# A mask addition moved from VectorE to TensorE, and a layer norm fused on VectorE, in a four-layer decoder with a computed order

## The chip, the cores and the metric

The kernel runs on one core of a Trainium2 chip. A core has a matrix engine (TensorE, PE in the profile, with its weight loads as PEld), VectorE (DVE), ScalarE (ACT), GpSimd (POOL) and SyncE (SP), which here only issues transfers. Each engine works off its own queue in order, and they meet at semaphores. Operands lie in SBUF, an on-chip memory of 128 partitions; matmuls write to PSUM, which GpSimd does not use here.

The metric is the device time of one execution in microseconds, as the median of several runs.

## What is computed

A stream of 128 batches of 64 tokens of width 128 passes four layers. Each layer adds an attention over a context and then a feed-forward part, both on a layer-normed stream:

```python
x = x + _L0_xattn_ref(_layernorm(x), ctx, ctx, mask_if1, ...)   # 16 heads of 8, mask per query and key
x = x + _L0_ffn_ref(_layernorm(x), ...)                          # 8 experts, all computed, gated
x = x + _L1_xattn_ref(ctx, _layernorm(x), mask_bk0, ..., rel_bias)
x = x + _L1_ffn_ref(_layernorm(x), ...)
x = x + _L2_xattn_ref(...)                                       # products without softmax
x = x + _L2_ffn_ref(...)                                         # one of 7 experts a token
x = x + _L3_xattn_ref(_layernorm(x), ctx, ctx, mask_bss, gamma, beta)
x = x + _L3_ffn_ref(...)                                         # attention with mixed weights
```

The change touches two places. In layer 0's attention the scores of masked pairs are set to a very negative value ahead of the softmax:

```python
scores = jnp.einsum('bhqd,bhkd->bhqk', query, key_) / np.sqrt(D_K)
scores = jnp.where(mask == 0, jnp.float32(NEG), scores)
attn = jax.nn.softmax(scores, axis=-1)
```

Layer 3's attention ends in a layer norm with a learned scale and shift:

```python
xhat = (x - mu) * jax.lax.rsqrt(var + EPS)
return xhat * gamma + beta
```

## The kernel before

**Groups and parts.** The 128 batches are cut into 16 groups of 8 batches (512 tokens). A group's stream lies in a tile of 128 partitions by 4 by 128, `xg[g]`, that stays in SBUF from start to end. For each group there are parts: `attention(g, 0)`, `l0f`, `attention(g, 1)`, `l1f`, `attention(g, 2)`, `route`. Layer 2's feed-forward part sorts tokens by expert (`table`, `block`, `shared`, `gather`) in two halves, groups 0 to 11 and 12 to 15. Then come `l3x` (layer 3's attention) for each group, `mix` for each four groups and `l3f` for each group.

**The order.** The program does not issue its instructions in the order in which it is written. Each piece of work is an `op` with an engine (or two to choose from), a planned duration, the tiles that it reads and writes, and a priority. `Plan.order` runs a model of five queues: for each engine it takes, among the ops that could start within `WINDOW` of the earliest one, the one of lowest priority number, and gives tiles their buffers as they come free. Where an op may go to two engines, `ALT` weighs the duration that it has on each. The number of buffers of each kind is in `spec`. A table `PRI` adds an offset to the priority of each kind of op. The result is a fixed order of each engine's queue. The planned durations are no more than the planner's: on the chip an instruction takes what it takes, and waits for semaphores.

**Layer 0's attention** (`attention`). A mask tile of 128x256 int32 is loaded (`load_mask`); POOL turns it into 0 or a very negative number in a tile `mb` (L933). Two projections give queries and keys. The keys are spread into a block-diagonal tile `kbd` by transfers (`fill_kbd`). For each half `v` of a group, `scores` (L733 on) issues 16 matmuls into the one PSUM tile `S` (four banks, 128x2048), L755. Two DVE instructions then add the mask while they move the scores to the SBUF tile `s` (L967). Then come the row maximum on DVE (`maximum`, L779), its subtraction on POOL (`shift`, L794), exp on ACT (`exp_`, L785), transposes on PE (`attend`, L809), the copy out of PSUM (`copy_out`, L593 on ACT or L591 on DVE), the product with the values (L821) and the normalisation on DVE (`normalise`, L837 to L845). `out_proj` (L888, L893) adds the outcome to the stream.

For layer 1, `scores` already has a way to add a mask on PE: it issues eight matmuls of a row of ones with the mask in bf16 (L743) ahead of the others, which then accumulate onto them.

**Layer 0's feed-forward part** (`l0f`) multiplies with all experts (L1068) and sums them on DVE (L1078). **Layer 1's** (`l1f`) has L1125 and L1144 on PE.

**Layer 3.** `l3x` computes scores, softmax and values for a group, then the statistics of the result (`stats`, L536 and L538), the reciprocal deviation on POOL (`pow_rs`, L544 and L545), and the norm: four tensor_scalar on DVE (L1562), a multiplication by gamma on POOL (L1570), the addition of beta to the stream (`add_row`, L610), and the addition of the product to the stream on POOL (L1574), and the stream's statistics for the next part. `gather` holds scalar_tensor_tensor instructions of 128x128 (L1464). `mix` picks experts for four groups (`choose`, `weigh`). `l3f` loads a pair of weight tiles for each batch (`load`; L1734 is the matmul that waits for them), and runs an attention much like layer 0's; for its second half, ACT copies the scores out of PSUM (L1786).

`route` ranks tokens: `r2` to `r5` are sequences of small DVE instructions (`r3` is L1211 to L1213), between `r3` and `r4` stands a count on PE (L1220).

Of the kernel before, what the change touches and what calls it, by code (L numbers as in the profile page):

```python
# [20 lines left out]
P = 128  # L21
# [44 lines left out]
SKEW, SKEW3, ALT, WINDOW = 15.0, 12.0, 1.160527449, 0.268996472  # L66
# [5 lines left out]
    "block0 block <lambda> 4": -4, "block0 block tr 0": 37, "block0 dma fn 4": 30.5,  # L72
    "block0 swiglu <lambda> 0": 3.5, "block0 swiglu <lambda> 1": 35.5, "block0 swiglu <lambda> 2": -1,
    "block0 swiglu down 0": 20, "block1 block <lambda> 1": 13.5, "block1 block <lambda> 4": -12.5,
    "block1 block tr 0": -22.5, "block1 dma fn 4": 71, "block1 swiglu <lambda> 0": 4,
    "block1 swiglu <lambda> 1": 41, "block1 swiglu <lambda> 2": -32, "block1 swiglu down 0": 1,
    "gather0 gather <lambda> 3": 3.5, "gather0 gather fn 2": 6.5, "gather0 stats fn 2": -0.5,
    "gather1 gather <lambda> 3": 78, "gather1 gather fn 2": 29.5, "gather1 stats fn 2": -3.5,
    "l0f copy_out fn 1": 3, "l0f l0f <lambda> 0": 9, "l0f l0f <lambda> 1": 9.5, "l0f l0f <lambda> 2": -145,
    "l0f l0f acc 2": -123.5, "l0f l0f eb 0": 46.5, "l0f l0f g1 2": 43.5, "l0f l0f g2 2": 41.5,  # L80
    "l0f ln_xn fn 1": 17.5, "l0f logits fn 0": 18.5, "l0f pow_rs fn 3": -4, "l0f stats fn 2": -39,
    "l0f transpose4 fn 0": 59.5, "l1f add_row <lambda> 3": 12.5, "l1f copy_out fn 1": -43.5,
    "l1f l1f <lambda> 0": 196, "l1f l1f <lambda> 2": 55.5, "l1f l1f <lambda> 3": 48, "l1f l1f choose 2": 11.5,
    "l1f l1f down 0": 360, "l1f l1f relu 1": 32, "l1f ln_xn fn 1": -12, "l1f logits fn 0": 5, "l1f pow_rs fn 3": 7,
    "l1f stats fn 2": 0.5, "l1f transpose4 fn 0": 45.5, "l3f0 attend av 0": 41.5, "l3f0 attend tr 0": -4.5,
    "l3f0 copy_out fn 1": -52, "l3f0 dma fn 4": -9.5, "l3f0 exp_ <lambda> 1": 25, "l3f0 fill_kbd fn 4": 56,
    "l3f0 l3f <lambda> 1": 2, "l3f0 l3f <lambda> 2": 17, "l3f0 l3f <lambda> 3": 106, "l3f0 l3f b_v 3": 51.5,
    "l3f0 l3f evac 1": -131, "l3f0 l3f load 4": -2, "l3f0 l3f project 0": -36.5, "l3f0 l3f put 2": -15,
    "l3f0 maximum fn 2": 40, "l3f0 normalise fn 2": 4, "l3f0 out_proj <lambda> 2": 36, "l3f0 out_proj fn 0": 11,
    "l3f0 scores fn 0": -58, "l3f0 shift fn 3": -1, "l3f1 attend av 0": 1, "l3f1 attend tr 0": -22,  # L90
    "l3f1 copy_out fn 1": 8.5, "l3f1 dma fn 4": -3, "l3f1 exp_ <lambda> 1": 14, "l3f1 fill_kbd fn 4": -18,
    "l3f1 l3f <lambda> 1": -2, "l3f1 l3f <lambda> 2": -13.5, "l3f1 l3f <lambda> 3": 4, "l3f1 l3f b_v 3": 9.5,
    "l3f1 l3f evac 1": 12.5, "l3f1 l3f load 4": -13.5, "l3f1 l3f project 0": -58, "l3f1 l3f put 2": -8,
    "l3f1 maximum fn 2": 4, "l3f1 normalise fn 2": -2, "l3f1 out_proj <lambda> 2": 4, "l3f1 out_proj fn 0": -4.5,
    "l3f1 scores fn 0": -26, "l3f1 shift fn 3": -6.5, "l3x0 add_row <lambda> 3": 8, "l3x0 copy_out fn 1": -36,
    "l3x0 dma fn 4": 61.5, "l3x0 l3x <lambda> 1": 166, "l3x0 l3x <lambda> 2": -5.5, "l3x0 l3x <lambda> 3": -10.5,
    "l3x0 l3x av 0": 28.5, "l3x0 l3x norm 2": -21.5, "l3x0 l3x sc 0": 7, "l3x0 l3x sums 2": 33,
    "l3x0 l3x tr 0": -17.5, "l3x0 ln_xn fn 1": 14, "l3x0 pow_rs fn 3": 12, "l3x0 stats fn 2": 9,
    "l3x0 transpose4 fn 0": 15, "l3x1 add_row <lambda> 3": 3.5, "l3x1 copy_out fn 1": -38, "l3x1 dma fn 4": 97,
    "l3x1 l3x <lambda> 1": 36.5, "l3x1 l3x <lambda> 2": 8, "l3x1 l3x <lambda> 3": -2, "l3x1 l3x av 0": 13.5,  # L100
    "l3x1 l3x sc 0": 26, "l3x1 l3x sums 2": -28.5, "l3x1 l3x tr 0": 7.5, "l3x1 ln_xn fn 1": -1,
    "l3x1 pow_rs fn 3": -3, "l3x1 stats fn 2": -1, "l3x1 transpose4 fn 0": -1, "mix0 add_row <lambda> 3": 26.5,
    "mix0 copy_out fn 1": -64, "mix0 ln_xn fn 1": -3.5, "mix0 mix <lambda> 0": 54.5, "mix0 mix <lambda> 1": 18.5,
    "mix0 mix <lambda> 2": -29.5, "mix0 mix b3mm 0": 37.5, "mix0 mix choose 2": 81, "mix0 mix put 2": 27.5,
    "mix0 mix spread_ 0": 101, "mix0 mix weigh 2": -76, "mix0 pow_rs fn 3": -17.5, "mix0 transpose4 fn 0": 38,
# [29 lines left out]
    "x2 stats fn 2": -15.5, "x2 transpose4 fn 0": 29, "x2 vproj_by_batch evac 2": -93.5,  # L135
    "x2 vproj_by_batch fn 0": -44, " b2_row b2_row 2": 2.5, " dma fn 4": 497, " lambda <lambda> 0": 32.5,
    " lambda <lambda> 2": -29.5, " lambda <lambda> 3": 14.5, " rel_mm rel_mm 0": -11.5,
    " scale_bq scale_bq 2": -1.5, " setup setup 3": 2.5, " stats fn 2": -18.5, " vset vset 2": 20,
}


# [1814 lines left out]
```

## Time and profile before

| | |
|---|---|
| median of 3 runs | 1987.3 us (1986.98 to 1990.2) |
| the profiled execution, its own time | 1991.25 us |
| its span | 1989.5 us |
| mean granted TensorE clock | 0.97 |
| busy: PE | 1811.3 us, 91% of the span |
| busy: DVE | 1546.2 us, 78% |
| busy: ACT | 1084.5 us, 55% |
| busy: POOL | 1022.3 us, 51% |

Durations in the next sections come from the one profiled execution. In a line of a group of instructions, the columns are: line of the program, engine, operation, output and inputs by tile name, shapes, number, and after the bar the busy time in us and the mean of one in ns, then the engine's idle time just before them and what ended most of it. In a line of waits: engine, output and line of the one that waited, what it waited for, total us, times, and the longest. In a line of the timeline: start, length, engine, line, operation. A busy time counts moments in which anything of the group ran, so overlapping matmuls count once.

### The profile page before, as it was taken

What the parts mean: (1) busy time and instruction counts of PE and PEld (TensorE: products, weight loads), DVE (VectorE), ACT (ScalarE), POOL (GpSimd) and SP (SyncE); (2) the same over time, 40 slices, a digit from 0 to 9 for tenths busy, and PEclk for the clock granted to TensorE, in tenths of its full rate; (3) what the DMA queues carried; (4) which work ended last, traced back from release to release, by engine and by line L of the source; (5) the groups of instructions that cost most, each with busy time, mean ns of one, the idle gap of its engine ahead of it and who ended that gap; (6) DMA issues with size and microseconds to landing.
All of it is one profiled execution on the core that took longest, in us unless ns stands there. A gap on an engine that the chain in (4) does not pass through costs nothing.

```text
span 1989.5 us, 66420 instructions
## 1 busy us (share of the span) xinstructions
PE 1811.3 (91%) x27506; PEld 1306.3 (66%) x27506; DVE 1546.2 (78%) x4023; ACT 1084.5 (55%) x2032; POOL 1022.3 (51%) x1331
## 2 busy tenths in 40 slices
PE   6878999999999999999999999999999897888886
PEld 5544756665765666765666677878756676677665
DVE  5989897878798987798887865354577877988776
ACT  2544755555655564556564554344455666765664
POOL 4635745554555664457654471020388767755231
PEclk8989999999999999999999999999999999998898
DMA  6200001011011010001101012444424576545561
GB/s 187 79 13 27 27 26 30 13 30 41 19 34 46 24 35 29 27 26 50 29 25 33 22 37 84 124 136 122 119 74 124 153 237 198 173 148 167 174 196 55
DMA packets 139229, 158.73 MB, mean 80 GB/s; under 512 B 40836, under 2 KB 98096, under 8 KB 138928
## 3 DMA queue, kind: packets, MB, share of 16 engines
q1 hardware_dynamic: 134832, 146.09, 24.2%
q0 software_dynamic: 4096, 8.40, 1.4%
q8 instruction: 216, 3.54, 0.8%
q14 instruction: 85, 0.70, 0.1%
HBM read 121.66 MB, written 15.99 MB: 69 GB/s over the span
## 4 chain that ended last, share of the span: by engine, by line
PE 50%; DVE 25%; POOL 7%; issue 7%; ACT 5%; DMA 4%; SPq 2%; POOLq 0%; DVEq 0%; ACTq 0%
PE b L1353 8%; PE b L1144 6%; PE b L809 5%; DVE x L1078 4%; POOL s L794 4%; DVE mx L779 4%; PE S L755 4%; PE b L1125 4%; PE b L1382 4%; PE b L1068 3%; PE b L638 3%; PE b L1734 3%; PE b L821 2%; PE b L864 2%; DVE s L967 2%
## 5 line engine op out<-in xcount | busy, mean ns | idle before, releaser
L794 POOL TENSOR_TENSOR s<-s,mx 128x512 f32<-128x512 f32 x320 | 324.0, 1047 | 224.1 <-DVE mx L779 190.5
L593 ACT COPY p<-b 128x512 f32<-128x512 f32 x370 | 199.4, 591 | 143.2 <-PE b L809 128.2
L809 PE MATMUL b<-ident,s 128*128 128x128 f32 x1536 | 217.1, 291 | 45.9 <-ACT s L785 33.7
L785 ACT ACTIVATE s<-s 128x2048 f32<-128x2048 f32 x96 | 183.8, 1914 | 114.2 <-POOL s L794 84.2
L809 PEld LDWEIGHTS b<-ident,s 128*128 128x128 f32 x1536 | 180.2, 149 | 91.0 <-ACT s L785 55.2
L563 ACT ACTIVATE xn<-x,nmr,rstd 128x128 f32<-128x128 f32 x472 | 194.4, 487 | 26.8 <-POOL nmr L548 25.2
L1078 DVE SCALAR_TENSOR_TENSOR x<-b,gt,x 128x128 f32<-128x128 f32 x512 | 177.8, 347 | 30.5 <-PE b L1068 14.3
L544 POOL TENSOR_SCALAR ve<-mv 128x4 f32<-128x4 f32 x144 | 34.8, 242 | 319.4 <-DVE mv L538 304.8
L755 PE MATMUL S<-kbd,q 32*64 32x256 f32 x4096 | 152.8, 404 | 42.6 <-DMA kbd<-k 20.4
L1144 PEld LDWEIGHTS b<-fw,hbig 128*128 128x128 f32 x1536 | 180.6, 195 | 10.4 <-issue 9.4
L1144 PE MATMUL b<-fw,hbig 128*128 128x128 f32 x1536 | 186.3, 279 | 0.0
L779 DVE TENSOR_REDUCE mx<-s 128x32 f32<-128x2048 f32 x80 | 181.8, 2274 | 3.6 <-ACT s L1786 2.9
L1370 DVE TENSOR_TENSOR hbig<-fm,b 128x256 f32<-128x256 f32 (+2 forms) x180 | 85.4, 487 | 102.0 <-ACT fm L1365 75.1
L1134 ACT ACTIVATE hbig<-b,cols 128x512 f32<-128x512 f32 x164 | 111.3, 685 | 82.8 <-PE b L1125 81.8
L1068 PE MATMUL b<-mats,fx 128*128 128x512 f32 x256 | 140.5, 632 | 1.9 <-DVE x L1078 1.5
L545 POOL TENSOR_TENSOR rstd<-ve,mhalf 128x4 f32<-128x4 f32 x128 | 133.6, 1044 | 10.6
L755 PEld LDWEIGHTS S<-kbd,q 32*64 32x64 f32 x4096 | 82.1, 137 | 83.2 <-DMA kbd<-k 19.2
L1353 PE MATMUL b<-fx,hbig 128*128 128x256 f32 (+1 forms) x528 | 129.1, 393 | 4.7 <-ACT fx L1441 1.0
L1365 ACT ACTIVATE fm<-b 128x256 f32<-128x256 f32 (+2 forms) x180 | 76.7, 438 | 101.0 <-PE b L1353 91.9
L821 PEld LDWEIGHTS b<-p,vaug 128*32 128x32 f32 x6144 | 97.1, 111 | 50.6 <-issue 23.5
L821 PE MATMUL b<-p,vaug 128*32 128x64 f32 x6144 | 123.3, 225 | 6.5 <-issue 3.6
L1125 PE MATMUL b<-fm,fw 128*128 128x512 f32 x256 | 125.1, 606 | 0.6 <-DVE x L1078 0.3
(292 smaller groups left out, 3870.2 us busy)
## 6 DMA issues: line engine op xcount, KB each, us to landing
fw<-in_l_w SPq DMA_DIRECT2D x64, 384.0 KB
vaug<-in_l_w SPq DMA_DIRECT2D x64, 384.0 KB
hbig<-in_l_w SPq DMA_DIRECT2D x44, 544.0 KB
c<-in_ctxT SPq DMA_DIRECT2D x64, 256.0 KB
kbd<-k SPq DMA_DIRECT2D x256, 64.0 KB
q<-xs_d SPq DMA_DIRECT2D x44, 128.0 KB
ys_d<-o SPq DMA_DIRECT2D x44, 128.0 KB
x<-in_x SPq DMA_DIRECT2D x32, 128.0 KB
```

What stands on the lines that cost most here:

```text
L563: A.activation(y[:, t, :], xg[g][:, t, :], AF.Identity, bias=nmr[:, g, n], scale=rstd[:, g, n])
L593: A.copy(tl(dst), tl(b))
L755: T.matmul(ps[64 * i : 64 * i + 64, r, u * 256 : u * 256 + 256], lhsT=qT[row, 64 * b : 64 * b + 64], rhs=kbd[row, :, 64 * b : 64 * b + 64] ...
L779: V.tensor_reduce(tl(mxr), heads(y), AX.X, ALU.max)
L794: G.tensor_tensor(y, y, bc(tl(mxr)[:, h], 2, [P, n, S]), ALU.subtract)
L809: T.transpose(tl(b)[:, r * P : (r + 1) * P], tl(s)[:, c : c + P], ident)
L821: T.matmul(tl(po)[32 * r : 32 * r + 32, c : c + 64], lhsT=vaugs[kv.slot][:, w0 : w0 + 32], rhs=tl(ps[p])[:, r * P + 64 * i : r * P + 64 * ...
L1068: lambda t=t, u=u, pe=pe: T.matmul(tl(pe), lhsT=tl(xnT)[:, t * P : (t + 1) * P], rhs=mats[:, M_E0 + 4 * u : M_E0 + 4 * u + 4, :], start=Tr ...
L1078: V.scalar_tensor_tensor(xg[g][:, t, :], tl(pe)[:, e * D : (e + 1) * D], w[:, t, 4 * u + e : 4 * u + e + 1], xg[g][:, t, :], ALU.mult, ALU ...
L1125: lambda n=n, src=src, ph=ph: T.matmul(tl(ph), lhsT=fw[:, n * P : (n + 1) * P], rhs=tl(src), start=True, stop=True),
L1144: T.matmul(tl(py)[:, t * P : (t + 1) * P], lhsT=tl(hs[n])[:, t * P : (t + 1) * P], rhs=w2f[:, n, :], start=(n == 0), stop=(n == 11),)
L1353: T.matmul(tl(ps)[0:n, at : at + m], lhsT=w()[:, off + c * P : off + c * P + n], rhs=tl(xT)[:, 0:m], start=True, stop=True,)
```

## The change

Layer 0's attention, for groups 0 to 4 only (`FIRST = 5`): POOL writes the mask as bf16; `scores` first issues four matmuls of the bf16 identity with the mask (one for each bank of `S`, 512 columns each, the mask's two blocks of 64 keys repeated over four heads by the access pattern), and the 16 score matmuls accumulate onto them; one ACT copy moves the sum to SBUF in place of the two DVE additions. Groups 5 to 15 stay as they were.

Layer 3's norm: the shift by beta is issued ahead; then for each of four token blocks two scalar_tensor_tensor instructions on DVE, (y - mean) * gamma and (that) * rstd + x. The two POOL instructions go.

The planner's inputs change too: planned durations of `r2`, `r3`, `r4`, `r5`, `av`, `choose`, `evac` and the latency of `load`; `ALT`, `WINDOW`; buffer counts; and the whole table `PRI` of offsets (left out here).

```diff
+FIRST = 5
-SKEW, SKEW3, ALT, WINDOW = 15.0, 12.0, 1.160527449, 0.268996472
+SKEW, SKEW3, ALT, WINDOW = 15.0, 12.0, 1.5, 0.237474501
...
+    ident_bf = sb("ident_bf", [P, P], BF16)
...
-        "c": (2, [P, GT]), "q": (2, [P, GT]), "k": (3, [P, GT]), "o": (3, [P, GT]),
-        "xnT": (1, [P, GT]), "xn": (2, [P, GT]), "fx": (2, [P, GT]), "fm": (4, [P, GT]), "p": (5, [P, GT]),
-        "s": (2, [P, 2048]), "m": (2, [P, 256]), "mb": (3, [P, 256]), "mx": (12, [P, 32]), "tn": (1, [P, 288]),
-        "st": (4, [P, TP * 6]), "gt": (2, [P, 264]),
+        "c": (2, [P, GT]), "q": (2, [P, GT]), "k": (3, [P, GT]), "o": (2, [P, GT]),
+        "xnT": (2, [P, GT]), "xn": (2, [P, GT]), "fx": (2, [P, GT]), "fm": (4, [P, GT]), "p": (5, [P, GT]),
+        "s": (2, [P, 2048]), "m": (3, [P, 256]), "mb": (2, [P, 256]), "mx": (7, [P, 32]), "tn": (1, [P, 288]),
+        "st": (8, [P, TP * 6]), "gt": (2, [P, 264]),
...
         make_identity(nc, ident)
+        G.tensor_copy(ident_bf, ident)
...
-    def scores(q, kv, kb, v, pri, keymask=None):
+    def scores(q, kv, kb, v, pri, keymask=None, pairmask=None):
...
+            if pairmask is not None:
+                pm = tl(pairmask).bitcast(BF16)[:, 0 : TP * S].rearrange("p (t k) -> p t k", k=S)
+                for r in range(4):
+                    T.matmul(
+                        ps[:, r, :], lhsT=ident_bf, rhs=bc(pm[:, 2 * v : 2 * v + 2, :], 2, [P, 2, 4, S]),
+                        start=True, stop=False,
+                    )
...
-                            start=keymask is None,
-                            stop=keymask is None or u == 1,
+                            start=alone,
+                            stop=alone or u == 1,
...
-        op(PE, 1.05 if keymask is None else 1.25, fn, r=[q, kb, *extra], w=[sc], hold=[kv], pri=pri, mode="s")
+        alone = keymask is None and pairmask is None
+        extra = [] if alone else [pairmask if keymask is None else keymask, C]
+        op(PE, 1.05 if alone else 1.25 if pairmask is None else 2.0, fn, r=[q, kb, *extra], w=[sc], hold=[kv], pri=pri, mode="s")
...
+        on_pe = layer == 0 and g < FIRST
...
-                lambda: G.tensor_scalar(tl(mask), tl(m).bitcast(I32), 0.0, NEG, ALU.is_equal, ALU.mult),
+                lambda: G.tensor_scalar(
+                    tl(mask).bitcast(BF16)[:, 0 : TP * S] if on_pe else tl(mask), tl(m).bitcast(I32), 0.0, NEG,
+                    ALU.is_equal, ALU.mult,
+                ),
...
-            if layer == 0:
+            if on_pe:
+                op(
+                    ACT, 1.95, lambda sc=sc, s=s: A.copy(tl(s), tl(sc).rearrange("p r c -> p (r c)")),
+                    r=[sc], w=[s], pri=pri,
+                )
+            elif layer == 0:
...
-        op(DVE, 1.1 + 0.45 * m, r2, r=[C], w=[rt], pri=pri)
+        op(DVE, 1.1 + 0.65 * m, r2, r=[C], w=[rt], pri=pri)
...
-        op(DVE, 0.2 + 0.8 * m, r3, w=[rt, RUN[half]], pri=pri - 1)
+        op(DVE, 0.2 + 1.0 * m, r3, w=[rt, RUN[half]], pri=pri - 1)
...
-        op(DVE, 0.7 + 0.4 * m, r4, r=[rank, W["misc2"]], w=[rt], p=[POS[half]], pri=pri - 1)
+        op(DVE, 0.6 + 0.2 * m, r4, r=[rank, W["misc2"]], w=[rt], p=[POS[half]], pri=pri - 1)
...
-        op(DVE, 1.4 + 0.2 * m, r5, w=[rt, *WSH[g0 : g0 + m]], pri=pri)
+        op(DVE, 1.1 + 0.1 * m, r5, w=[rt, *WSH[g0 : g0 + m]], pri=pri)
...
-        op(PE, 1.0, av, r=[pT, cv], w=pos_, hold=[y], pri=pri, mode="v")
+        op(PE, 0.65, av, r=[pT, cv], w=pos_, hold=[y], pri=pri, mode="v")
...
+        add_row(g, R_BETA, pri)
+
         def norm():
             for t in range(TP):
-                V.tensor_scalar(
-                    g4(tl(y))[:, t, :], g4(tl(y))[:, t, :], mv3[:, g, t, 0:1], rs3[:, g, t : t + 1],
-                    ALU.subtract, ALU.mult,
+                y_, x_ = g4(tl(y))[:, t, :], xg[g][:, t, :]
+                V.scalar_tensor_tensor(
+                    y_, y_, mv3[:, g, t, 0:1], rows[:, R_GAMMA : R_GAMMA + D], ALU.subtract, ALU.mult
                 )
-
-        op(DVE, 1.3, norm, r=[R3, M3], w=[y], pri=pri, port=True)
-        op(
-            POOL, 1.27,
-            lambda: G.tensor_tensor(g4(tl(y)), g4(tl(y)), bc(rows[:, R_GAMMA : R_GAMMA + D], 1, [P, TP, D]), ALU.mult),
-            r=[W["rows"]], w=[y], pri=pri,
-        )
-        add_row(g, R_BETA, pri)
-        op(POOL, 1.27, lambda: G.tensor_tensor(xg[g], xg[g], g4(tl(y)), ALU.add), r=[y], w=[X[g]], pri=pri)
+                V.scalar_tensor_tensor(x_, y_, rs3[:, g, t : t + 1], x_, ALU.mult, ALU.add)
+
+        op(DVE, 1.75, norm, r=[R3, M3, W["rows"]], w=[y, X[g]], pri=pri)
...
-        op(DVE, 4.2, choose, r=[W["rows"], C], w=[sel, pg], pri=pri)
+        op(DVE, 2.7, choose, r=[W["rows"], C], w=[sel, pg], pri=pri)
...
-                op(SP, 0.95, load, r=[TAB3[g // GATE]], w=[wt], pri=pri - 1, lat=3.5, after=[*mark["l1f"], *mark["x2"]])
+                op(SP, 0.95, load, r=[TAB3[g // GATE]], w=[wt], pri=pri - 1, lat=4.3, after=[*mark["l1f"], *mark["x2"]])
...
-            op(ACT, 0.5, evac, r=[b, *VA], p=[va], hold=[kv], pri=pri, alt=[(DVE, 0.5)])
+            op(ACT, 0.6, evac, r=[b, *VA], p=[va], hold=[kv], pri=pri, alt=[(DVE, 0.5)])
```

## The prediction

> **What bounds the kernel now.** I read three views. First the busy time of each engine by stretch, for the span is not one regime. Columns: stretch and its length, busy us of PE, PE weight load, DVE, ACT, POOL (records in brackets), granted TensorE clock, DMA share, GB/s.
>
> ```profile
> 33.00:200.00 167.00, 133.71 (x1785) 79.26 (x1781) 152.70 (x412) 81.39 (x131) 88.96 (x126) 0.90 0.18 53
> 200.00:1450.00 1250.00, 1207.92 (x17307) 852.29 (x17306) 956.72 (x2390) 669.85 (x1237) 599.23 (x777) 0.99 0.16 47
> 1450.00:1820.00 370.00, 318.08 (x5035) 247.20 (x5035) 306.11 (x963) 229.51 (x483) 270.42 (x348) 0.95 0.53 161
> 1820.00:1989.50 169.50, 128.84 (x3089) 108.92 (x3083) 118.49 (x213) 95.41 (x169) 50.00 (x54) 0.91 0.46 146
> ```
>
> From 200 to 1450 us PE is busy 96.6% of the time: it is the bound, and what another engine does there is worth little. From 33 to 200 us it is the other way round: DVE 91%, PE 80%, ACT 49%. In the last 540 us nobody is full (PE 83%, DVE 79%).
>
> Second, the chain that ended last, its pieces added up by engine for each stretch. From 33 to 200 us: DVE 96.5 us, PE 36.0, POOL 13.9, issue 10.7, ACT 10.6. From 250 to 1450 us: PE 758, DVE 291, the rest 161. It agrees: DVE rules the start.
>
> Third, the groups of instructions by shape. In the start stretch:
>
> ```profile
> L1078 DVE SCALAR_TENSOR_TENSOR x<-b,gt,x 128x128 f32<-128x128 f32 x125 | 43.2, 345 | 5.8 <-PE b L1068 2.4
> L779 DVE TENSOR_REDUCE mx<-s 128x32 f32<-128x2048 f32 x12 | 27.2, 2270 | 0.0
> L967 DVE TENSOR_TENSOR s<-S,mb 128x1024 f32<-128x1024 f32 x20 | 23.7, 1207 | 4.4 <-PE S L755 4.4
> ```
>
> L967 is the mask addition of layer 0. All 20 of these in the stretch are four for each of groups 0 to 4, between 35.0 and 189.5 us. These are exactly the ones that the change takes from DVE.
>
> **Part 1: the mask of layer 0.** Removed: 20 x 1.207 = 24.1 us of DVE.
>
> Added on PE: ten times four matmuls (128x128 bf16 weights, 512 columns). The trace has no such matmul. The nearest is L743, which adds layer 1's mask from bf16 with 512 columns:
>
> ```profile
> 1011.97 0.42 PE L743 MATMUL S<-mb,ones_bf 1*64 1x512 bf16 x8
> 1012.21 1.05 PE L755 MATMUL S<-kbd,q 32*64 32x256 f32 x32
> ```
>
> The first column is the start, the second the length. The next group starts 0.24 us after L743's. L743's eight matmuls use eight different parts of the array (four row groups by two column halves), so I read 0.24 us as one shared pass of 512 columns. L1125, f32 with 512 columns, leaves two records a matmul, 0.475 us from start to start, so 0.95 us a matmul. The new matmuls fill the array and cannot share a pass: 4 x 0.24 = 0.96 us, ten times = 9.6 us of PE. Bounds: 2.4 us in all if the four shared one pass as L743's do, 4 x 0.95 x 10 = 38 us if they cost as L1125's. I take 9.6, since L743 has the type and the columns.
>
> Added on ACT: ten copies of 128x2048 out of PSUM. Layer 3 has that copy: L1786, 1.860 us, so 18.6 us. ACT then has 100 of 167 us. The POOL operation that builds the mask writes bf16 in place of f32: 1.093 us now (L933); L939, with a bf16 output of twice the columns, takes 1.945, so nothing changes. The copy of the identity to bf16 in the setup is POOL work of at most some 0.3 us (the two instructions that build ident take 0.20 and 0.29), before a POOL idle of 3.40 us: nothing.
>
> The single S buffer is held about as long: now 1.12 (PE) + 2.36 (two adds), then 2.08 + 1.86, so 0.5 us more, ten times, in a stretch where PE has 33 us of idle time.
>
> What it is worth: engines work their queues in order, so I price each moved microsecond by its engine's share of the chain in this stretch. DVE: 24.1 x 96.5/167 = -13.9. PE: 9.6 x 36.0/167 = +2.1. ACT: 18.6 x 10.6/167 = +1.2. Sum **-10.6 us**. Ends: PE has 133.7 + 9.6 = 143.3 us of work; at the 97.3% that it reaches from 200 to 250 us the stretch would last 147.3, so no more than -19.7; if DVE's relief bought nothing and all PE work came on top, +9.6. What is late next is PE, which after 200 us sets the pace, so time won here stays won.
>
> **Part 2: layer 3's norm.** Now four tensor_scalar on DVE, a multiplication by gamma and an addition to x on POOL; then eight scalar_tensor_tensor on DVE.
>
> ```profile
> L1562 DVE TENSOR_SCALAR o<-o,mv,rs 128x128 f32<-128x128 f32 x64 | 26.5, 477 | 2.9 <-POOL rs L545 2.9
> L1570 POOL TENSOR_TENSOR o<-o,rows 128x512 f32<-128x512 f32 x16 | 20.5, 1280 | 14.0 <-DVE o L1562 14.0
> L1574 POOL TENSOR_TENSOR x<-x,o 128x512 f32<-128x512 f32 x16 | 20.3, 1271 | 0.9
> L1464 DVE SCALAR_TENSOR_TENSOR x<-k,tok,x 128x128 f32<-128x128 f32 x64 | 22.5, 412 | 0.0
> 1461.18 1.13 DVE L1464 SCALAR_TENSOR_TENSOR x<-k,tok,x 128x128 f32<-128x128 f32 x4
> ```
>
> L1464 is the new instruction's like: same operation, size and both tensors in SBUF. Undisturbed, four take 1.13 us, so one each 0.26 us and 0.08 at the end; eight take 2.2. The four of L1562 take 1.11 undisturbed (1.68 on average, as some are stretched to 1.4 us beside POOL). So DVE gains 1.07 us a group, 17 us over 16 groups, and POOL loses 40.8.
>
> On the chain between 1490 and 1820 us lie 8.0 us of L1562 (five groups' worth) and 5.1 us of L1570 and L1574 (two groups' worth). 5 x 1.07 = 5.4 comes, 5.1 goes: **0 us**. Ends: -13 if both lines leave the chain, +17 if every added microsecond is on it. The cover of the first is that DVE has 64 us idle in this stretch; without it the +17 holds.
>
> [...]
>
> **Part 3: the order.** Every queue's order is computed from a list of offsets, costs and buffer counts, and all three change. The offsets have no row to be priced by, but the costs can be held against the trace. At four groups, r2: planned 2.9, now 3.7; measured 3.7 (592.65 to 596.35). r3: 3.4 to 4.2; 4.1. choose: 4.2 to 2.7; 2.4. av: 1.0 to 0.65; 0.67. All nearer. Where PE pays for a wrong one:
>
> ```profile
> PE b L1220 <- DVE rt L1213: 4.7, 2, 2.4
> PE b L1734 <- DMA vaug<-in_l_w: 4.0, 7, 1.2
> PE b L1734 <- DMA fw<-in_l_w: 1.9, 4, 1.0
> ```
>
> That is 4.7 us for the routing sums in the PE-bound stretch and 5.9 us for layer 3's weights, whose assumed latency goes from 3.5 to 4.3 us. SP's queue gets no new transfer; only the places of its old ones move. Between 0 and -10.6; I take half, **-5 us**. What the offsets do beyond that has no row; the rivals hold it.
>
> **Sum.** -10.6 + 0 - 5 = -16 us. The profiled execution took 1991.25 us (span 1989.5 and 1.75 around it), 4 us above the median of 1987.3: 1975 by its time, **1971** by the median.
>
> **Rivals.**
> *The start does not shrink.* DVE's queue gets shorter, but PE waits there also for exp (11.1 us, L809 on ACT) and for kbd transfers (3.9 us), and ACT, which does exp, gets the copies. If these take DVE's place, only part 3 or less remains: 0 to -5, some 1985. For it: ACT's copies stand in the queue ahead of exp. Against: ACT at 60% has room.
>
> *PE's density in the middle falls (slower).* The new order has two buffers for attention outputs in place of three and seven for maxima in place of twelve, so between 200 and 1450 us three interleaved layers must let each other pass sooner, and PE waits at out_proj and scores. The lowest 50-us slice there has 92.3%. Midway between that and 96.6%, at 94.4%, the 1208 us of PE work take 1279: +30, net +14, 2001. It decides from 95.4%, where the 16 us are eaten up. Against it: each "kv" buffer carries one attention and there are two, so a third output buffer was seldom of use, and the second xnT buffer frees the layer norms.
>
> *The end packs better too.* After 1450 us PE idles 93 us. With POOL rid of 41 us, the new order could fill a quarter: -23 more, 1948. For it: layer 3's maxima, shifts and weight loads alternate there without any engine being full. Against: the last group's chain of exp, shift and transpose has nothing to overlap with.
>
> **How the numbers follow.** Forecast 0.50 (its own range 1959 to 1982); start does not shrink 0.14; PE less dense 0.20; end packs better 0.16. Within 0.2% (4 us), about what a measurement of this kernel tells from no change, lies half of the second case: 0.07. Faster 0.50 + 0.16 + 0.07 = 0.73; slower 0.20. The range goes from below 1948 to the middle of the slow case, 1943 to 2000; that leaves out half of the slow case, 0.10, and 0.06 below.
>
> **What would show it.** Right: 44 records of L967's line left and 26 copies of PSUM to 128x2048 on ACT; PE's new matmuls with starts 0.24 us apart; DVE's share of the chain before 200 us below 58%, and group 5's first mask addition (227.8 now, if the order keeps it) or the first layer-1 FFN earlier by some 10 us; the eight norm instructions in about 2.2 us. Wrong: PE's share from 200 to 1450 us under 95.4%; new matmuls 0.9 us apart; a stretch up to 200 us that is as long as now with PE waiting for ACT.

## The result, and the profile after

The changed kernel takes 2001.2 us (median of 8 runs, 1996.4 to 2012.7) where the kernel before takes 1987.1 us beside it: a ratio of **1.0084, interval 1.0058 to 1.0109**. It is slower: the ratio goes by the means, which lie 17 us apart (the medians lie 14 apart); the forecast was 16 us faster. The profiled execution took 2012.69 us, the longest of the eight, with a span of 2010.9 and a mean granted clock of 0.962; that of before has 1989.5 and 0.97.

First the stretches that the prediction was made from, now of the changed kernel (stretch and length, busy us of PE, weight load, DVE, ACT, POOL, then granted clock, DMA share, GB/s):

```profile
33.00:200.00 167.00, 142.88 (x2021) 87.29 (x2020) 144.89 (x422) 100.04 (x143) 95.45 (x139) 0.89 0.18 53
200.00:1450.00 1250.00, 1212.63 (x17109) 852.37 (x17108) 933.47 (x2359) 670.31 (x1238) 574.41 (x745) 0.99 0.16 47
1450.00:1820.00 370.00, 309.26 (x4685) 243.20 (x4684) 320.04 (x960) 228.17 (x481) 229.87 (x314) 0.93 0.53 158
1820.00:2010.90 190.90, 144.21 (x3436) 120.12 (x3434) 146.61 (x290) 104.95 (x186) 60.35 (x68) 0.91 0.43 137
```

The start moved the way that was forecast: DVE is down by 8 us and PE up by 9, and DVE's part of the chain there falls from 96.5 to 69.4 us (42% of the stretch). Of the two dates named ahead, group 5's first mask addition comes 15 us earlier (213.0 for 227.8), but the first matmul of layer 1's feed-forward part 16 us later (213.0 for 196.5): the new order mixes the layers in another way, so single dates don't tell what was won. The middle is as dense as it was, 97.0% for 96.6. The end got worse: between 1450 and 1820 us DVE has 14 us more and PE 9 us less, and the last stretch is 21 us longer.

Busy shares don't say when work is done. So I counted PE's matmul records by line and shape up to a given time, weighed each with its shape's busy time per matmul in one run of the changed kernel, and left the new mask matmuls out. That gives the us of common PE work done by then, good to 2 or 3 us between two kernels, as it depends on how matmuls at the cuts are counted. Main pair, before and after: at 200 us 153.4 and 156.6; at 1450, 1555.1 and 1555.3; at 1550, 1656.6 and 1655.2; **at 1600, 1710.5 and 1690.8**; at 1820, 1945.1 and 1928.6. So some 3 us are won in the start and lost again by 1450 us, and 18 us go in the single stretch from 1550 to 1600.

There the two changes meet. First DVE's queue (start, length, engine, line, operation), the new norm of one group with the feed-forward product "hbig" behind it; then what POOL does beside it:

```profile
1568.94 1.18 DVE L1589 SCALAR_TENSOR_TENSOR x<-o,rs,x 128x128 f32<-128x128 f32 x1
1570.04 0.34 DVE L1586 SCALAR_TENSOR_TENSOR o<-o,mv,rows 128x128 f32<-128x128 f32 x1
1570.41 0.35 DVE L1589 SCALAR_TENSOR_TENSOR x<-o,rs,x 128x128 f32<-128x128 f32 x1
1570.68 3.33 DVE L1586 SCALAR_TENSOR_TENSOR o<-o,mv,rows 128x128 f32<-128x128 f32 x1
...
1574.97 1.07 DVE L1391 TENSOR_TENSOR hbig<-fm,b 128x256 f32<-128x256 f32 x3
```
```profile
1570.13 1.21 POOL L1475 DMA_INDIRECT k<-ys_d,ypos  x1 [0.16 <-issue]
1571.38 2.48 POOL L612 TENSOR_TENSOR x<-x,rows 128x512 f32<-128x512 f32 x2
```

An instruction that takes 0.34 us two lines earlier takes 3.33 beside POOL's two row additions: it ends 0.15 us after the second of them. It starts 0.70 us ahead of the first, beside the end of a DMA_INDIRECT that the two instructions before it passed undisturbed; what held it until the additions began is not shown. The group's norm lasts from 1568.1 to 1575.0, and only then does DVE get to hbig. Next PE's queue, and the same microseconds as windows of 5 us:

```profile
1569.74 0.23 PE L1628 MATMUL b<-gws,mats 128*32 128x4 f32 x2
1575.44 1.11 PE L585 MATMUL b<-ident,xn 128*128 128x128 f32 x4 [5.47 <-DVE hbig L1391]
```
```profile
1565.00:1570.00 5.00, 4.84 (x22) 3.18 (x22) 4.82 (x15) 4.69 (x14) 3.32 (x5) 1.00 0.78 226
1570.00:1575.00 5.00, 0.00 (x0) 0.00 (x0) 4.89 (x8) 2.29 (x4) 3.69 (x3) 0.84 0.22 66
1575.00:1580.00 5.00, 4.56 (x22) 4.23 (x25) 4.21 (x25) 1.34 (x3) 0.23 (x1) 0.50 0.00 0
```

PE stands still for 5.47 us, and then works 5 us at a granted clock of 0.50: the gap is paid twice (the four matmuls of L585 at 1575.44 take 1.11 us, the four at 1605.70, where the clock is 1.00, take 0.66). The next norm, 1585.7 to 1591.2, stands ahead of hbig as well; PE waits 4.60 us, and the clock of the row around the end of that wait, 1590 to 1595, is 0.55. From 1550 to 1600 PE is busy 35.6 us at a mean clock of 0.80; before, 44.2 at 0.98. Over the whole span the clock withheld, span x (1 - clock), is 2010.9 x 0.038 = 76.4 us after and 59.7 before, 16.7 us more at a span 21.4 us longer. But that is the slowest of eight executions: over the eight it runs from 47.9 to 76.4, and the one that took 1999.6 us has 57.9, less than the profiled one of before. So these two holes cost clock as well, and the clock goes with the spread between executions of one kernel; the loss as a whole does not follow it.

The groups that the change touches, first from 33 to 200 us, then over the whole run (count | busy us, mean ns | idle before):

```profile
L981 ACT COPY s<-S 128x2048 f32<-128x2048 f32 x10 | 18.7, 1869 | 8.1 <-PE S L764 8.1
L743 PE MATMUL S<-mb,ident_bf 128*128 128x512 bf16 x40 | 11.2, 406 | 3.0 <-ACT s L981 2.0 <-DVE s L999 0.8 <-POOL mb L944 0.2
```
```profile
L988 DVE TENSOR_TENSOR s<-S,mb 128x1024 f32<-128x1024 f32 x44 | 52.4, 1215 | 2.6 <-PE S L764 2.5
L1586 DVE SCALAR_TENSOR_TENSOR o<-o,mv,rows 128x128 f32<-128x128 f32 x64 | 33.7, 526 | 0.0
L1589 DVE SCALAR_TENSOR_TENSOR x<-o,rs,x 128x128 f32<-128x128 f32 x64 | 32.1, 502 | 6.7 <-POOL rs L547 3.7
```

44 of L988 (L967 before) are left, 10 copies of L981 are new, and the mask's matmuls cost about what was priced (11.2 us busy for 9.6): four last 1.04 us at 39.25, and the next group of PE starts 0.97 us after the first of them, 0.24 each. The norm does not: 33.7 + 32.1 = 65.8 us of DVE for the old 26.5, so +39 where +17 was priced.

### The profile page after: what moved, and what is told of

Same layout as the page of the kernel before. It is cut to its first block, busy times and chain, and to the rows that moved or that the text cites. A ratio compares the mean times of both kernels' runs of the same rounds, so it can differ in the third digit from the quotient of the medians.

```text
span 2010.9 us, 66529 instructions
## 1 busy us (share of the span) xinstructions
PE 1833.5 (91%) x27546; PEld 1322.2 (66%) x27546; DVE 1558.2 (77%) x4080; ACT 1110.1 (55%) x2058; POOL 973.9 (48%) x1294
## 4 chain that ended last, share of the span: by engine, by line
PE 55%; DVE 25%; POOL 6%; issue 6%; ACT 4%; DMA 2%; SPq 1%; DVEq 0%; POOLq 0%; ACTq 0%
PE b L1165 8%; PE b L1374 8%; PE b L1146 5%; PE b L819 5%; PE b L1403 5%; POOL s L804 4%; DVE mx L789 4%; DVE x L1099 3%; PE S L764 3%; PE b L640 3%; PE b L898 3%; PE b L831 2%; PE b L1089 2%; PE b L874 2%; PE b L585 2%
## 5 line engine op out<-in xcount | busy, mean ns | idle before, releaser
L595 ACT COPY p<-b 128x512 f32<-128x512 f32 x357 | 190.7, 592 | 135.0 <-PE b L819 128.2
L565 ACT ACTIVATE xn<-x,nmr,rstd 128x128 f32<-128x128 f32 x492 | 201.8, 486 | 45.6 <-POOL nmr L550 44.4
L1165 PEld LDWEIGHTS b<-fw,hbig 128*128 128x128 f32 x1536 | 176.5, 192 | 12.0 <-issue 8.6
L1165 PE MATMUL b<-fw,hbig 128*128 128x128 f32 x1536 | 178.2, 275 | 0.7 <-DVE x L1099 0.7
L764 PE MATMUL S<-kbd,q 32*64 32x256 f32 x4096 | 146.4, 395 | 20.1 <-DMA kbd<-k 11.4
L1089 PE MATMUL b<-mats,fx 128*128 128x512 f32 x256 | 147.8, 661 | 4.6 <-DVE x L1099 2.9
L1155 ACT ACTIVATE hbig<-b,cols 128x512 f32<-128x512 f32 x154 | 105.6, 686 | 73.1 <-PE b L1146 71.7
L1270 POOL DMA_INDIRECT xs_d<-p,rt x64 | 64.4, 1006 | 132.0 <-DVE p L569 119.6
```

The source lines that it names most:

```text
L565: A.activation(y[:, t, :], xg[g][:, t, :], AF.Identity, bias=nmr[:, g, n], scale=rstd[:, g, n])
L595: A.copy(tl(dst), tl(b))
L764: T.matmul(ps[64 * i : 64 * i + 64, r, u * 256 : u * 256 + 256], lhsT=qT[row, 64 * b : 64 * b + 64], rhs=kbd[row, :, 64 * b : 64 * b + 64] ...
L1089: lambda t=t, u=u, pe=pe: T.matmul(tl(pe), lhsT=tl(xnT)[:, t * P : (t + 1) * P], rhs=mats[:, M_E0 + 4 * u : M_E0 + 4 * u + 4, :], start=Tr ...
L1165: T.matmul(tl(py)[:, t * P : (t + 1) * P], lhsT=tl(hs[n])[:, t * P : (t + 1) * P], rhs=w2f[:, n, :], start=(n == 0), stop=(n == 11),)
```

## The experiments

They ran on four chips, on which the kernel before took 1992 to 2042 us. So each is given as the ratio to the kernel before, run beside it on the same chip, with its interval. "Old order" and "new order" are the queues of the kernel before and of the changed kernel. Instructions were exchanged in place, inside an operation of the planner whose cost and buffers were left alone, so the rest of every queue stays as it was.

### One part alone, in the old order

**b_norm_new**: the new norm.

```diff
-                V.tensor_scalar(g4(tl(y))[:, t, :], ..., ALU.subtract, ALU.mult)
+                V.scalar_tensor_tensor(y_, y_, mv3[:, g, t, 0:1], rows[:, R_GAMMA : R_GAMMA + D], ALU.subtract, ALU.mult)
+                V.scalar_tensor_tensor(x_, y_, rs3[:, g, t : t + 1], x_, ALU.mult, ALU.add)
...
-            lambda: G.tensor_tensor(g4(tl(y)), g4(tl(y)), bc(rows..., ALU.mult),
+            lambda: None,
...
-            lambda: G.tensor_tensor(xg[g], xg[g], g4(tl(y)), ALU.add)
+            lambda: None
```

> The old order of every queue, with the new norm put in the place of the old one: eight scalar_tensor_tensor where four tensor_scalar stood, and the two POOL instructions left out. Theory N (the norm's cost on VectorE): the eight took 2.75 us a group undisturbed in the changed kernel's trace (not the 2.2 forecast), and instructions next to POOL's were stretched to 1 to 3 us, 65.8 us of busy time in all where 26.5 stood; in the last 540 us VectorE becomes the bound, so 1995 to 2005 us against 1987. Theory O (the order of the new list is to blame, not the instructions): 1984 to 1990. Theory M (the mask on TensorE is to blame): 1984 to 1990 too.

Measured 1.0046 [1.0029, 1.0063]: **+9.4 us**. Eight instructions a group cost DVE 25.3 + 26.8 = 52.1 us here, not 65.8: how far they are stretched depends on what POOL does beside them (in micro, below, sixteen such instructions take 4.3 us alone and 17.1 beside POOL's SBUF additions), and that is the order's doing.

**b_mask_new**: the mask of groups 0 to 4 on PE, the copy on ACT.

```diff
+            if pairmask is not None:
+                for r in range(4): T.matmul(ps[:, r, :], lhsT=ident_bf, rhs=bc(pm..., 2, [P, 2, 4, S]), start=True, stop=False)
...
-                        lambda u=u, ...: V.tensor_tensor(..., ALU.add)
+                        lambda u=u, ...: ((A.copy(tl(s), ...) if u == 0 else None) if on_pe else V.tensor_tensor(..., ALU.add))
...
-        "mx": (12, [P, 32])
+        "mx": (11, [P, 32])
```

> The old order of every queue, with the mask of groups 0 to 4 added by TensorE and the sum copied by ScalarE in the places where VectorE's additions stood; one buffer of maxima less, for room, which leaves the order as it was. Theory M: TensorE is handed 11.2 us and has nothing to gain, 1992 to 1998 us against 1987. Theories N and O: VectorE's relief of 24 us in the first 200 us wins something, 1977 to 1984. If nothing comes of it: 1985 to 1989.

Measured **0.9968 [0.9953, 0.9983], -6.5 us**, the fastest kernel of the study: it beats both. Against b_norm_new, whose start is that of the kernel before, on the same chip, it has 6.2 us more PE work done at 200 us and 4.3 at 1450. From 33 to 200 us DVE is busy 139.7 us for 154.8, and the granted clock is 0.97 for 0.90. So part 1 works, by about the amount seen at 200 us; how much of that is the clock's is not shown.

### Both parts in the old order, and the changed kernel again

**b_both_new** has both edits above in the old order; **after_again** is the changed kernel, unedited, on the same chip.

> The old order of every queue with the new instructions of both parts. If the parts add: 0.9968 + 0.0046, so 0.999 to 1.004 of the time before. If the changed kernel's loss lay in the instructions: 1.006 or more.

> The changed kernel, unedited, beside the others of this set, so that all stand on one chip. 1.006 to 1.011 of the time before, as first measured.

b_both_new 1.0021 [0.9992, 1.0049], after_again 1.0072 [1.0044, 1.0101]. The same instructions cost 0.5%, 10 us, more in the new order (the intervals of the two ratios overlap by a little; the kernels stood side by side on one chip, with medians of 2043.2 and 2056.4 us). PE work done, b_both_new and after_again: at 1450 us 1525.5 and 1531.7, at 1550 1628.8 and 1628.6, at 1650 1730.9 and 1714.4. The new order is ahead until 1500 us and loses 23 us from there to 1650, where the main pair loses them too.

### One part undone, in the new order

**a_norm_old**, **a_mask_old** and **a_both_old** put the old instructions in the places of the new ones; the DVE additions stand where ACT's copy was planned.

```diff
-                V.scalar_tensor_tensor(y_, ...); V.scalar_tensor_tensor(x_, ...)
+                V.tensor_scalar(y_, y_, mv3[:, g, t, 0:1], rs3[:, g, t : t + 1], ALU.subtract, ALU.mult)
+            G.tensor_tensor(g4(tl(y)), ..., ALU.mult); G.tensor_tensor(xg[g], xg[g], g4(tl(y)), ALU.add)
```

> The changed kernel's order of every queue, with the old norm in the place of the new one: four tensor_scalar on VectorE, then the product with gamma and the addition on POOL at the same place. Theory N: VectorE loses 39 us of busy time and 10 to 20 us come back, 1981 to 1991 us. Theory O: 1998 to 2004, as POOL's two instructions also stand in a queue that was not made for them. Theory M: 1998 to 2004.

> The changed kernel's order of every queue, with the mask of groups 0 to 4 added by VectorE where ScalarE's copy stood, and no mask matmuls. Theory M: 1988 to 1996 us. Theories N and O: part 1 is worth something, so it gets slower than the changed kernel's 2001: 2004 to 2012. If part 1 does nothing: 1998 to 2004.

> The changed kernel's order of every queue with the old instructions of both parts in it, so the order alone. Theory O, as the four runs so far suggest (old order: mask 0.9968, norm 1.0046; new order: without the norm 1.0096, without the mask 1.0139): 1.011 to 1.017 of the time before. If the parts explain the loss by themselves (theory N): 0.996 to 1.004.

a_norm_old 1.0096 [1.0067, 1.0125], a_mask_old 1.0139 [1.0119, 1.0159], a_both_old 1.0146 [1.0106, 1.0185]. With old instructions in both, the new order with its buffers costs **1.5%, 30 us**. a_norm_old and a_mask_old are slower than any of the theories had it. Part 1 is worth 0.5 to 0.7% in it (1.0146 to 1.0096, and 1.0139 to 1.0072; both pairs lie across two chips, and the intervals of the first overlap). Part 2 has no cost here that stands clear of the noise (1.0096 to 1.0072, 1.0146 to 1.0139). Yet the hole behind hbig is the new norm's: after 1450 us PE waits for hbig 20.8 us in after_again, 20.6 in a_mask_old, 6.9 in a_norm_old and 7.5 in a_both_old. The two longest of these lines in after_again, then in a_norm_old (total, times, longest):

```profile
PE b L1403 <- DVE hbig L1391: 7.7, 4, 4.6
...
PE b L585 <- DVE hbig L1391: 6.8, 2, 5.5
```
```profile
PE b L1403 <- DVE hbig L1391: 4.4, 4, 2.1
...
PE b L585 <- DVE hbig L1391: 1.0, 1, 1.0
```

But the loss only moves: a_norm_old has a clock of 0.98 from 1550 to 1600 us, and 0.82 from 1600 to 1650. That this order was planned for a norm that leaves POOL alone is a likely reason, not a tested one.

### The dependence inside the norm

**a_norm_split** is the changed kernel with the four first steps of a group ahead of the four second ones, so that no instruction reads what the one before it wrote.

```diff
+            for t in range(TP):
+                y_, x_ = g4(tl(y))[:, t, :], xg[g][:, t, :]
                 V.scalar_tensor_tensor(x_, y_, rs3[:, g, t : t + 1], x_, ALU.mult, ALU.add)
```

> The changed kernel, but with the four first steps of the norm ahead of the four second steps, so that no instruction follows the one whose result it reads. Theory N: 0.27 us from start to start in place of 0.38 and 0.27 in turn, 2.2 us a group in place of 2.75, 9 us of VectorE in all; 3 to 6 us of it on the path, 0.998 of the changed kernel's time. Theory O: within 0.1% of the changed kernel.

1.0051 [1.0034, 1.0068], against 1.0072 [1.0044, 1.0101] of after_again on the same chip. The sign is as the shorter spacing would have it, and PE waits for hbig 14.5 us after 1450 in place of 20.8, but the intervals overlap: inconclusive. The two steps still take 30.9 + 27.3 = 58.2 us of DVE, for 65.1 in after_again.

### The order computed anew

Four kernels are the changed one with planner inputs of the kernel before, and a new order from them: **h_pri1_old** has the old offsets up to the routing, **h_pri2_old** those of the stages behind it, **h_prices_old** the old planned durations and latency, **h_all_old** all old inputs.

```diff
-        op(DVE, 1.1 + 0.65 * m, r2, r=[C], w=[rt], pri=pri)
+        op(DVE, 1.1 + 0.45 * m, r2, r=[C], w=[rt], pri=pri)
...
-        op(PE, 0.65, av, r=[pT, cv], w=pos_, hold=[y], pri=pri, mode="v")
+        op(PE, 1.0, av, r=[pT, cv], w=pos_, hold=[y], pri=pri, mode="v")
```

> The changed kernel with the other half of the offsets old: those of the stages up to route, with the last stages' new ones. Theory O2: the loss stays, and the 7 us gained ahead of 1450 us go too: 1.007 to 1.014 of the time before. If the first stages' offsets are to blame: 1.000 or less.

> The changed kernel; of the table of offsets, the entries of the stages table, block, shared, gather, l3x, mix and l3f are the old ones, and the order is computed anew. Counted in TensorE work done, the new order was 7 us ahead at 1450 us and fell 22 us back between 1500 and 1650. Theory O2 (the offsets of the last stages do it): the 22 us come back, 0.994 to 1.000 of the time before. If other inputs of the planner do it (buffers, ALT, WINDOW, planned durations): 1.005 to 1.010, as the changed kernel.

> The changed kernel with the old planned durations of r2 to r5, av, choose, evac and the old latency of load; offsets, buffers, ALT and WINDOW new, the order computed anew. The prediction put -5 us on the new ones, for they are nearer to the trace: then 1.009 to 1.012 of the time before. If nearer prices are worth nothing by themselves: within 0.4% of the changed kernel either way, with no sign foretold.

> The new instructions of both parts with all of the planner's old inputs, the order computed anew with the new operations' own planned durations. If the inputs matter and not the computing anew: as the old order with both parts in place, 0.999 to 1.005 of the time before. If any new computation of the order costs as much as the change did, because offsets fit one set of operations alone: 1.008 or more.

1.0475 [1.0446, 1.0504], 1.0475 [1.0446, 1.0505], 1.0561 [1.0533, 1.0589] and 1.0444 [1.0409, 1.0480]. Every one costs some 90 us or more; only h_all_old lies where one of its theories had it (1.008 or more), the others far above theirs. So in these four an offset or a planned duration has no value of its own: the list of offsets fits one set of operations, costs and buffers, and each mixture tried gives a far worse order. They can't tell whether durations nearer to the trace would help a list of offsets made for them, nor which input the new order loses by; for that the order itself had to be carried over.

### The order carried over

The planner can be made to follow a written list: each operation gets its place, and the first one in the list that has its inputs and buffers is taken.

```diff
+        line = sorted(self.ops, key=lambda o: o.at)
...
-                cands, lo = [], None
-                for o in ready[e]:
+            for o in line:
+                if left[o]: continue
...
+                best = (0, t, e, o)
+                break
```

**s_ab** has the new order up to 1425 us of planned time and the old one behind it, **s_ba** the reverse, both with new instructions and the new buffer counts; **s_ab_old** is s_ab with the old norm. By the traces VectorE's first 2789 instructions of s_ab, to 1441 us, are the changed kernel's in its order, and its first 2784 of s_ba, to 1451 us, those of b_both_new.

> The changed kernel with its own order for everything that it plans to start before 1425 us (planned time), and from there the order of the kernel before, carried over operation by operation (with the changed kernel's buffers and both new instructions). Theory E (the order of the end carries the loss: the changed kernel was 7 us of PE work ahead at 1450 us and lost 22 between 1500 and 1650): ratio to before 0.996 to 1.000. Rival S (the loss belongs to the order and the buffers of the first 1425 us, or to the buffers in the end): 1.004 to 1.008, as the changed kernel.

> The reverse: the order of the kernel before for what it plans to start before 1425 us, then the changed kernel's order, with both new instructions and the changed kernel's buffers. Theory E: 1.006 to 1.012 (the old start is 7 us behind, the new end is kept). Rival S: 0.998 to 1.003.

> As s_ab, but layer 3's norm as before (four tensor_scalar on VectorE, two tensor_tensor on GpSimd) in the place of the new one. If part 2 costs 9 us in the old order of the end, as in the pair without and with it there: 0.0045 below s_ab, so 0.991 to 0.996, the fastest of all. If in this order it costs nothing or gains, as in the changed kernel's own order: equal to s_ab or above it.

s_ab 1.0189 [1.0165, 1.0212], s_ba 1.0106 [1.0078, 1.0134], s_ab_old 1.0120 [1.0100, 1.0139]. Theory E, that the order of the end alone carries the loss, **fell**: the old end on the new start is the slowest of the three. What holds: the new start is ahead (6.6 us of PE work at 1450, s_ab over s_ba), the new end has its hole again (s_ba's clock is 0.80 from 1550 to 1600, as in the main pair), and in the old end the new norm costs 0.7%, for the 0.5% that it costs in the old order. But s_ab, 17 us ahead of s_ba at 1650, is 7 behind at 1820. It has the old end on the new buffer counts, which led to the last pair.

**s_bb** has the old order with the new buffer counts, **s_aB** the new order with the old ones (both with new instructions; where a buffer is missing, an operation comes later: in s_bb 3968 of VectorE's 4067 instructions still stand at their old place).

```diff
-        "o": (3, [P, GT]) "xnT": (1, [P, GT]) "m": (2, [P, 256]) "mb": (3, [P, 256]) "mx": (11, [P, 32]) "st": (4, [P, TP * 6])
+        "o": (2, [P, GT]) "xnT": (2, [P, GT]) "m": (3, [P, 256]) "mb": (2, [P, 256]) "mx": (7, [P, 32]) "st": (8, [P, TP * 6])
```

> Both new instructions in the old order of all queues, as b_both_new, but with the changed kernel's buffer counts (o 3 to 2, xnT 1 to 2, m 2 to 3, mb 3 to 2, mx 11 to 7, st 4 to 8); where a buffer is missing, an operation is put later (about 1% of the places in the end). Theory B (the old end needs the old buffers: s_ab, which had the old end on the new buffers, lost 17 us against it between 1700 and 1820): ratio 1.012 to 1.020. Rival C (s_ab lost at the seam between the two orders): 1.000 to 1.005, as b_both_new.

> The reverse: the changed kernel's order and instructions with the old buffer counts (mx 11); where a buffer is missing, an operation is put later. If the buffers, and not the order, are what part 3 lost by: 0.996 to 1.002. If the new order's own loss between 1500 and 1650 us does not come from the buffers: 1.004 to 1.008 or more, as the changed kernel, whose order was made for its own buffers.

| both new instructions | old buffer counts | new buffer counts |
|---|---|---|
| old order | 1.0021 [0.9992, 1.0049] (b_both_new) | 1.0168 [1.0145, 1.0191] (s_bb) |
| new order | 1.0391 [1.0356, 1.0426] (s_aB) | 1.0072 [1.0044, 1.0101] (after_again) |

The new counts alone cost the old order 1.5%; the new order wins 1% of that back, and on the old counts it is far worse than the old one. Order and buffers can't be priced apart. From 1550 to 1650 us, b_both_new, s_bb and after_again in this sequence:

```profile
1550.00:1650.00 100.00, 83.61 (x810) 64.73 (x808) 88.22 (x346) 64.67 (x155) 57.13 (x91) 0.98 0.59 174
```
```profile
1550.00:1650.00 100.00, 80.75 (x654) 61.78 (x656) 83.40 (x328) 59.10 (x136) 53.58 (x88) 0.90 0.48 142
```
```profile
1550.00:1650.00 100.00, 77.31 (x702) 60.87 (x701) 82.73 (x294) 49.88 (x117) 62.80 (x92) 0.88 0.45 129
```

With the new counts the old order loses PE time and clock in the same 100 us as the new order does. The waits of PE after 1450 us that grew most from b_both_new to s_bb (total, times, longest) are those behind layer 3's score tiles "mb", of which there are two in place of three; first b_both_new, then s_bb:

```profile
PE b L1455 <- DVE mb L1522: 4.7, 3, 1.9
...
PE b L820 <- DVE mb L1522: 2.5, 1, 2.5
```
```profile
PE b L2008 <- DVE mb L1783: 7.8, 1, 7.8
...
PE b L1716 <- DVE mb L1783: 6.0, 3, 2.5
```

All lines of this kind together have 8.9 us and 20.6 us. Two things limit this. By PE work done, s_bb falls some 12 us behind b_both_new between 1550 and 1650 us and another 23 between 1750 and 1960, so the larger part comes later. And the new order waits there for something else: for "mb" only 1.7 us after 1450 in after_again, for hbig 20.8 (3.3 in b_both_new and in s_bb), and s_aB, the new order on the old counts, waits 23.4 us for hbig. So the hole of the new order is not made by the new counts. Which of the six counts costs the old order its 1.5% was not tried one by one, and stays open.

### The norm's instruction by itself

**micro** is the kernel before with a measurement behind its last instruction. Each line has sixteen 128x128 f32 instructions on DVE; POOL adds two 128x512 SBUF tensors beside three of them.

```diff
+        for i in range(16):
+            V.scalar_tensor_tensor(f_[0][:, w_[i]], p_[0][:, w_[i]], c_, p_[1][:, w_[i]], ALU.subtract, ALU.mult)
...
+        pool_two(12)
+        for i in range(16):
+            V.scalar_tensor_tensor(f_[0][:, w_[i]], bk[0][:, w_[i]], c_, p_[1][:, w_[i]], ALU.subtract, ALU.mult)
```

> The kernel before, with a measurement behind its last instruction (its own work is complete; the time of the run is not used). Sixteen scalar_tensor_tensor of 128x128 f32 alone, each independent of the one before: 0.26 us from start to start. Eight pairs in which the second reads the first's result: 0.38 and 0.27 alternately if the dependence makes the difference, 0.27 each if it was something else. Sixteen beside GpSimd tensor_tensor that read two SBUF tensors: theory P (VectorE and GpSimd share what they read SBUF through): 0.5 to 0.6 each; if the stretch came from something else, 0.26. The same with the first source in PSUM, and tensor_scalar with one SBUF source: by P little or no stretch; with GpSimd at memset: none.

The groups: L1870 alone, L1878 beside POOL, L1882 beside POOL with the first source in PSUM, L1886 tensor_scalar beside POOL, L1891 beside POOL's memset. Then two dependent pairs:

```profile
L1870 DVE SCALAR_TENSOR_TENSOR fm<-p,mv,p 128x128 f32<-128x128 f32 x16 | 4.3, 347 | 0.0
L1878 DVE SCALAR_TENSOR_TENSOR fm<-p,mv,p 128x128 f32<-128x128 f32 x16 | 17.1, 1144 | 0.0
L1882 DVE SCALAR_TENSOR_TENSOR fm<-b,mv,p 128x128 f32<-128x128 f32 x16 | 4.2, 342 | 0.0
L1886 DVE TENSOR_SCALAR fm<-p,mv 128x128 f32<-128x128 f32 x16 | 17.0, 1140 | 0.0
L1891 DVE SCALAR_TENSOR_TENSOR fm<-p,mv,p 128x128 f32<-128x128 f32 x16 | 4.3, 343 | 0.0
```
```profile
1997.31 0.34 DVE L1873 SCALAR_TENSOR_TENSOR fm<-p,mv,p 128x128 f32<-128x128 f32 x1
1997.69 0.35 DVE L1874 SCALAR_TENSOR_TENSOR fm<-fm,mv,p 128x128 f32<-128x128 f32 x1
1997.96 0.35 DVE L1873 SCALAR_TENSOR_TENSOR fm<-p,mv,p 128x128 f32<-128x128 f32 x1
```

Alone, one starts each 0.26 us ((4.28 - 0.35) / 15). Beside POOL sixteen take 17.1 us, **four times as long**, where theory P had put down a doubling; with the first source in PSUM, or with POOL only writing, they take 4.2 to 4.3. tensor_scalar with its one SBUF source, of which little or no stretch was expected, takes 17.0. The second of a pair starts 0.38 us after the instruction whose result it reads, the next pair 0.27 after that: the dependence costs 0.11 us. What VectorE and GpSimd share, which theory P names, is not shown. The source's place alone costs nothing here: sixteen with both sources in SBUF take 4.3 us alone, sixteen with the first in PSUM 4.2, even beside POOL.

## Why the prediction was wrong, step by step

**Part 1 was right in mechanism and sign.** -10.6 was forecast, with ends at -19.7 and +9.6; it measures -6.5 in the old order (-3.5 to -9.6) and about -10 to -14 in the new one. PE took the matmuls at 0.24 us each as priced. The statement that time won here stays won held in the old order (6.2 us ahead at 200, 4.3 at 1450), not in the main pair, where 3 us at 200 are 0 at 1450.

**Part 2 was mis-sized.** The step that failed: eight instructions at L1464's spacing, 2.2 us a group and +17 us of DVE. Undisturbed a group takes 2.75 us (the one below from 1671.12 to 1673.87), since every second instruction reads the result of the one before: it starts 0.38 to 0.45 us after that one, and the next 0.27 after it. The first three of such a group in the changed kernel:

```profile
1671.12 0.34 DVE L1586 SCALAR_TENSOR_TENSOR o<-o,mv,rows 128x128 f32<-128x128 f32 x1
1671.57 0.35 DVE L1589 SCALAR_TENSOR_TENSOR x<-o,rs,x 128x128 f32<-128x128 f32 x1
1671.84 0.34 DVE L1586 SCALAR_TENSOR_TENSOR o<-o,mv,rows 128x128 f32<-128x128 f32 x1
```

And most groups are disturbed (11 of the 16 hold an instruction of over 0.4 us): 65.8 us over 16 groups is 4.1 each. The kernel before had stretched ones as well (L1464's median is 343 ns, its longest 1520; L1562's are 340 and 1435), and the means that the prediction shows, 412 and 477 ns, hold them; but it priced the new instructions at undisturbed durations, and set the part at 0. It measures +9.4 us in the old order (+11 with the mask moved as well: 1.0021 over 0.9968, across two chips), inside its ends of -13 and +17.

**Part 3 failed, in sign and in its bounds.** "Between 0 and -10.6; I take half" gave no room for a loss. The order and the buffers cost +10 us with the new instructions and +30 with the old ones. "I take half" has no run behind it: putting the old planned durations back into the new list gives 5.6% above the kernel before, which shows a mismatch and not what nearer durations are worth. And "a third output buffer was seldom of use" was said of the middle, which stayed dense; no step asked what the order and the counts do to the end. There the new counts cost the old order 1.5%, and the new order puts the norm ahead of hbig. How the 10 us divide between the two stays open.

**The rivals.** The start shrank, so the first is out. PE's density in the middle was 97.0%, so the slower rival did not come: its number, 2001 us, is the measured one by luck. Its mechanism, fewer buffers, is seen in the old order's end, where PE waits for "mb"; that it makes the new order's loss is not shown. That the end packs better is the opposite of what came. The time lies 1 us above the range (1943 to 2000), by way of a case that it did not hold.

**What no step had** is the clock. The rows that the prediction shows have it: 0.90 in the start and 0.91 in the last stretch against 0.99 in the middle. It was 0.50 for 5 us behind the hole of 5.47 us, but it does not account for the loss. Averaged over all executions on one chip, after_again has 72.6 us withheld and the kernel before 78.2, though its spans are 14 us longer; b_norm_new has 75.6, as much as the kernel before, with spans 9.5 us longer. In b_mask_new both went down: 64.0, with spans 7 us shorter.

By ratios, in the old order: part 1 -0.3%, part 2 +0.5%, order and buffers +0.5%, together 0.7%; the main pair has 0.84% [0.58, 1.09].

## What to carry to other kernels

An order computed from offsets that fit one set of operations and buffers is part of the tuning: exchange an instruction inside it first, without computing it anew, and measure that alone; here it is 0.9968, while the four orders computed anew from mixed inputs cost 4 to 6%. Price an instruction that moves to VectorE by how it runs beside GpSimd's SBUF reads (here 17.1 us for sixteen, 4.3 alone), with its dependence on the one before (0.38 us from start to start, 0.27 to the next), and by what stands behind it in the queue. The gaps of TensorE of 4.60 and 5.47 us were paid twice here where they stand, once for themselves and once for the clock behind them (0.55 and 0.50); whether the whole run is longer by it has to be read from all executions, not from the profiled one.

## What was not expected of the hardware

- Sixteen scalar_tensor_tensor of 128x128 f32 take 17.1 us beside GpSimd's tensor_tensor on SBUF and 4.3 alone, and sixteen tensor_scalar with one SBUF source 17.0 beside it (four undisturbed ones of the old norm took 1.11), while twelve of GpSimd's 128x512 additions take 16.1 us beside these and 16.0 beside the form from PSUM: GpSimd loses 0.1 us by it at most.
- In micro a scalar_tensor_tensor of 128x128 f32 that reads the result of the one before it starts 0.38 us after it, an independent one 0.26.
- In the changed kernel the granted clock was 0.50 in the row of 5 us behind 5.47 us without a matmul, 0.67 in the row behind 4.02 us (1630.76 to 1634.78), and 0.63 and 0.68 in the two rows from 1555 to 1565, around and behind the end of 3.09 us (1554.35 to 1557.44); after 3.35 us (1602.35 to 1605.70) it stayed at 1.00, and in the kernel before at 1.00 in all rows from 1570 to 1600, with gaps of up to 0.86 us. How long a gap has to be for the clock to fall is not shown.
- The kernel before took from 1987 to 2042 us in the sets of runs, 2.7%, more than any effect of a part; two sets on one chip agree (2035.1 and 2034.2 us). So only ratios taken on one chip could be compared.
